# One chain of side stages through all scans, with spread loads and later transfers, in a four-layer scan and attention kernel

## The chip, the cores and the metric

The kernel runs on one core of a Trainium2 chip. A core has a matrix engine (TensorE, PE in the profile), three engines for elementwise work (VectorE or DVE, ScalarE or ACT, GpSimd or POOL), and SyncE (SP), which here issues nearly all transfers. Each engine takes its own instructions strictly in order and waits at an instruction until its semaphores allow it. The metric is the device time of one execution in microseconds (us); the median of several runs counts.

## The reference

The input `x` is 4 images of 96 channels and 64 by 64 pixels, in float32. Four layers follow each other for each image, each fed by a normalised copy of the running result and added to it:

- L0: attention of 3 heads from all 4096 pixels to 1024 pooled samples, a weighting of each pixel's 2 by 2 block by its 9 neighbouring samples, a 5 by 5 depthwise convolution and a projection.
- L1: a selective scan over the pixels in four orders, then a layer norm, a gate, 1x1, 3x3 depthwise and 1x1 convolutions, and a channel gate.
- L2: a 3 by 3 convolution with all 96 by 96 channels.
- L3: convolutions, again a selective scan in four orders, layer norms, a gate with a second branch, grouped convolutions and a softmax over channels.

The scans are the largest part. For each of 192 channels and 16 states, in each of four orders (rows, rows backwards, columns, columns backwards), both L1 and L3 compute, written as in L3,

```
step: h = h * exp(d[..., None] * A) + (d * uu)[..., None] * bb[:, :, None, :]
      y = einsum('bkdn,bkn->bkd', h, cc)
```

where `d`, `bb` and `cc` are themselves projections of the input at that pixel. The four orders' results are added. So there are 8 large scans: two layers by four images.

## The kernel before

The function `streams` does everything for these inputs (`general` is a second version that runs only where a range check fails). Its main loop runs through 8 scans in the order of `SCANS`: L1 of images 0 and 1, L3 of 0 and 1, L1 of 2 and 3, L3 of 2 and 3. A scan is cut into 32 groups (4 orders, or ways, x 4 chunks of 1024 pixels x 2 halves of 96 channels), and a group into `NG` = 12 units. A unit is a tile of 128 partitions (16 states x 8 channels) by 1024 pixels. There are 8 x 384 = 3072 units.

A unit `i` goes through the engines in steps, which the function `unit` emits for several units at once:

- `fetch` (L1964): SyncE loads the group's `dd` (the step sizes, stored to memory by `prepare`), repeated over the 16 states, into one of 12 `rep` buffers. It is emitted `AHEAD` = 4 units ahead.
- `decays` (L1971): ScalarE turns `rep` into exp(d*A), two units ahead.
- `drive` (L1978): TensorE spreads the group's `parts` into one of two `bx` tiles in PSUM (1024 columns), two units ahead; `times_b` (L1987): VectorE multiplies it by `bc`, one unit ahead.
- `scan` (L1991): VectorE runs the recurrence into `hs`; `carry_on`: ScalarE copies its last column to the next chunk's start.
- `times_c` (L2006): GpSimd multiplies `hs` by `bc` back into `rep`.
- `collect` (L2010): every fourth unit, TensorE sums the states of four units into `acc`, which takes one PSUM tile; after the last four of a group `output` (L2028) adds or copies `acc` into the tile `yo`, and its store to `y_row` or `y_col` is put into `store` and issued at the beginning of the next unit.

`prepare` (L1863) makes the inputs of a group two groups ahead, in steps that `unit` places one or two at a time: projections on TensorE, the softplus on ScalarE and GpSimd, and transfers through memory (`rows` to `bc`, `dd`, `du` to `parts`). Its transfers are emitted some units after the step that makes their data, through `later(n, f)`; it starts when `LEAD` = 6 units of a group are left.

Beside the scan, the same loop does the rest of the network. Each image has the stages `first` (L0 and the inputs of L1's scan), `second` (the rest of L1, L2 and the inputs of L3's scan), and `third` (the rest of L3); `last` is the `third` of the last image, which works while its own scan still runs. They are Python generators. A `Slots` object takes the next piece of a generator with `begin`, up to three times in a unit: before `decays`, between `times_b` and `collect`, and after `drive`. A piece is mostly some matmuls into a PSUM tile from `bank()`; where it yields `None`, `end` then emits what follows on the other engines, later in the same unit. TensorE's time of the pieces is estimated and subtracted from a budget: `PACE[s]` us per unit of scan `s`, less 0.43 for `drive` and 1.71 where `collect` is due. A piece that yields `WAIT` is not ready yet and takes the rest of that `begin`'s budget.

`BESIDE[s]` lists what runs beside scan `s`. A new `Slots` begins at each scan's first unit, and what is left of it 19 units before the scan's end is emitted at once. First(0) runs alone before the loop, and what is left of `last` after it: `solo` is true there, and the tiles of `bx` serve as banks.

PSUM has little room: `bx` 2 x 2 banks, `acc` 2 banks, and the tag `one` two banks, for `bank()` outside solo. `held()` takes one of these two for long: for the sums and weighted values in `attention`, the variance rows in `layer_norm`, the sums in `neighbours`. Meanwhile one bank is left for all pieces.

`directions` (L1440) begins `second` and `third`: for both halves it loads the column result `yc` and the row result `V` in 32 transfers of 96 KB, turns the columns with ScalarE (`turned`), and adds both on TensorE. `second` waits there (`stored[0] < full - 1 + h`) until its scan's stores are issued. `finish` (L1673) is the rest of `third` and `last`. In `group_norm_on_scalar` (L1095) ScalarE sums four pieces and VectorE reduces them; at L1619 and L1620 ScalarE's Tanh is followed by VectorE's product on the same bank; in `layer_norm` ScalarE's Sqrt is followed by VectorE's reciprocal.

## Time and profile before

| | before |
|---|---|
| median of 3 runs | 14276.35 us (14261.17 to 14285.1) |
| the profiled execution | 14250.58 us, its span 14248.7 us |
| PE, DVE, ACT, POOL busy | 81%, 82%, 61%, 72% |
| alone before the first unit, and after the last | 690.5 us, 127.4 us |
| scans 0 to 7 | 1660, 1646, 1630, 1604, 1590, 1624, 1633, 2044 us |
| transfers | 2694.85 MB, mean 189 GB/s |

Busy time is that of an engine's own instructions; issuing transfers and waiting for semaphores do not count. PEld is TensorE's weight load, which overlaps its matmuls. A row of the groups of instructions shows line, engine, operation, what is written and read, the count, then the busy time and the mean in ns, then the engine's idle time before them and what ended most of it. Windows give each engine's busy time in a stretch, with the granted TensorE clock (1.00 is full speed), the share of time in which the 16 DMA engines were busy, and GB/s. A row of waits names the waiting instruction, what ended its wait, the total in us, how often, and the longest. The helper `mm` issues every matmul, so all matmuls have its line, L964, and are told apart by their tiles.

### The profile page before, as it was taken

To read this page: it belongs to the slowest core of one execution; us is meant where nothing else is said; L and a number is where in the kernel's file an instruction comes from. 1 tells how busy PE (TensorE), PEld (TensorE's weight loads), DVE (VectorE), ACT (ScalarE), POOL (GpSimd) and SP (SyncE) were. 2 spreads that over 40 slices of the span, in tenths; PEclk is the share of its full clock that TensorE was granted. 3 is DMA by queue.
4 is the path that set the end of the run, shared out by engine and by line. 5 is a ranking of instruction groups with operands and counts; after the bars stand their busy time and mean duration, and the time that the engine had idled before them with its cause. 6 is when DMAs were issued, how large, how long until landed. Compare 5 with 4: busy or idle time off the path is not lost.

```text
span 14248.7 us, 127656 instructions
## 1 busy us (share of the span) xinstructions
PE 11588.7 (81%) x40137; PEld 3442.3 (24%) x40802; DVE 11635.9 (82%) x7509; ACT 8680.4 (61%) x12307; POOL 10197.3 (72%) x4637
## 2 busy tenths in 40 slices
PE   8878886988879796888868887988879797877767
PEld 2322321322213221222212221222213221211111
DVE  1478888987889888889988898897989888777786
ACT  3266566666756676665756566566756666655554
POOL 0167887877868777778877787787868777655573
PEclk9889887998879897999979997998879897777766
DMA  0267788787878888678977788787878878676684
GB/s 10 61 154 193 196 216 208 197 213 181 226 185 217 210 205 216 172 185 219 237 178 196 195 220 231 186 223 180 230 191 218 211 195 222 169 178 174 165 198 106
DMA packets 846672, 2694.85 MB, mean 189 GB/s; under 512 B 112480, under 2 KB 115008, under 8 KB 845984
## 3 DMA queue, kind: packets, MB, share of 16 engines
q1 hardware_dynamic: 845328, 2685.08, 74.9%
q8 instruction: 325, 5.32, 0.2%
q14 instruction: 363, 2.97, 0.1%
q10 hardware_dynamic: 656, 1.47, 0.0%
HBM read 2185.95 MB, written 500.17 MB: 189 GB/s over the span
## 4 chain that ended last, share of the span: by engine, by line
PE 36%; DVE 20%; ACT 15%; DMA 11%; issue 7%; POOL 7%; SPq 1%; DVEq 0%; POOLq 0%; ACTq 0%
PE one L964 24%; DVE hs L1996 12%; PE bx L964 6%; PE acc L964 6%; DVE bx L1989 6%; DMA rep<-dd 5%; ACT rep L1976 4%; POOL rep L2008 4%; ACT L1976 1%; DMA du<-cut 1%; PE held L964 1%; ACT ex L1309 1%; DMA parts<-du 1%; DMA yc<-ycol 1%; ACT L1918 1%
## 5 line engine op out<-in xcount | busy, mean ns | idle before, releaser
L2008 POOL TENSOR_TENSOR rep<-hs,bc 128x1024 f32<-128x1024 f32 x3072 | 7219.0, 2356 | 2792.8 <-DVE hs L1996 2410.8
L1996 DVE TENSOR_TENSOR_SCAN hs<-rep,carry,bx 128x1024 f32<-128x1024 f32 x2304 | 5401.2, 2344 | 301.6 <-ACT carry L2004 33.3
L1989 DVE TENSOR_TENSOR bx<-bx,bc 128x1024 f32<-128x1024 f32 x3072 | 3720.1, 1211 | 862.4 <-PE bx L964 616.7
L1976 ACT ACTIVATE rep<-rep,l_decay 128x1024 f32<-128x1024 f32 x3072 | 3497.0, 1143 | 879.3 <-DMA rep<-dd 851.6
L964 PE MATMUL bx<-parts,spread 128*128 128x512 bf16 x5479 | 1959.3, 434 | 1242.4 <-DVE hs L1996 1123.2
L1996 DVE TENSOR_TENSOR_SCAN hs<-rep,bx 128x1024 f32<-128x1024 f32 x768 | 1754.2, 2284 | 136.2 <-ACT carry L2004 56.1
L964 PE MATMUL acc<-rep,ct 128*32 128x512 f32 x12288 | 1833.1, 712 | 11.8 <-POOL rep L2008 8.7
L964 PEld LDWEIGHTS <-spread 128*128 128x128 bf16 x6144 | 458.6, 102 | 3655.5 <-DVE hs L1996 2239.6
L964 PE MATMUL one<-band,dg 96*96 96x512 f32 x2304 | 1067.0, 595 | 4.6 <-ACT band L1512 0.8
L964 PE MATMUL one<-upad,diag 96*96 96x512 f32 x2016 | 959.0, 607 | 6.9 <-ACT pr L1881 2.2
L964 PE MATMUL one<-qq,kk 96*128 96x512 f32 x1152 | 659.9, 656 | 201.4 <-ACT ex L1309 137.3
L964 PE MATMUL one<-pr,ct 6*96 6x512 f32 x1024 | 691.3, 761 | 69.9 <-ACT pr L1881 24.6
L964 PEld LDWEIGHTS acc<-rep,ct 128*32 128x32 f32 x12288 | 374.3, 123 | 1268.0 <-issue 1026.3
L1309 ACT ACTIVATE ex<-one 128x512 f32<-128x512 f32 x576 | 342.0, 594 | 548.5 <-PE one L964 547.0
L1976 ACT ACT_TABLE_LOAD x474 | 608.1, 1283 | 8.3
L964 PE MATMUL one<-hp,diag 96*96 96x512 f32 x1152 | 580.8, 641 | 35.6 <-POOL diag L1134 33.5
L964 PE MATMUL one<-vpad,diag 96*96 96x512 f32 x1200 | 579.2, 610 | 2.1
L2004 ACT COPY carry<-hs 128x1 f32<-128x1 f32 x2304 | 407.8, 177 | 225.5 <-DVE hs L1996 224.6
L964 PE MATMUL held<-ex,cols 128*32 128x256 f32 x3072 | 504.1, 404 | 18.1 <-ACT ex L1309 11.7
L964 PE MATMUL held<-ex,vT 128*32 128x256 f32 x3072 | 504.5, 405 | 0.0
L964 PEld LDWEIGHTS one<-band,dg 96*96 96x96 f32 x2304 | 368.8, 163 | 507.2 <-issue 426.1
L964 PEld LDWEIGHTS one<-upad,diag 96*96 96x96 f32 x2016 | 327.9, 165 | 456.3 <-issue 392.0
(3422 smaller groups left out, 14112.9 us busy)
## 6 DMA issues: line engine op xcount, KB each, us to landing
rep<-dd SPq DMA_DIRECT2D x3072, 512.0 KB
parts<-du SPq DMA_DIRECT2D x1024, 144.0 KB
bc<-rows SPq DMA_DIRECT2D x256, 512.0 KB
dd<-delta SPq DMA_DIRECT2D x256, 384.0 KB
du<-cut SPq DMA_DIRECT2D x256, 384.0 KB
yrow<-yo SPq DMA_DIRECT2D x128, 512.0 KB
ycol<-yo SPq DMA_DIRECT2D x128, 512.0 KB
us<-urow SPq DMA_DIRECT2D x128, 384.0 KB
```

The lines of the kernel that those rows point to most:

```text
L964: nc.tensor.matmul(o, lhsT=lhsT, rhs=rhs, start=first, stop=last)
L1309: nc.scalar.activation(last.rearrange("p a b -> p (a b)"), p, AF.Exp, scale=HD**-0.5)
L1918: nc.scalar.activation(w, w, AF.Ln)
L1976: nc.scalar.activation(a, a, AF.Exp, scale=decay[tag][:, k, NG * h + m : NG * h + m + 1])
L1989: nc.vector.tensor_mul(bx, bx, ready[i // NG][2][:, 0, :])
L1996: nc.vector.tensor_tensor_scan(out=hs, data0=a, data1=bx, initial=carry[:, h, m : m + 1] if c else 0.0, op0=ALU.mult, op1=ALU.add)
L2004: nc.scalar.copy(carry[:, h, m : m + 1], live[i][1][:, CH - 1 : CH])
L2008: nc.gpsimd.tensor_tensor(a, hs, ready[i // NG][2][:, 1, :], ALU.mult)
```

## The change

- `BESIDE`: third(0) and third(1) go beside scans 3 and 4, after first(2) and first(3). Beside scan 7 third(2) and `last` stay.
- The stages form one generator through all scans, in one `Slots`. A scan's end is no boundary: the next stage may begin in it. What is still open 19 units before a scan's end is emitted as before, but only up to the end of that scan's list (`done`).
- A clock counts units, and `stores` notes the unit in which each y store is issued. `landed(n)` is true two units after the n-th. `directions` first loads the image that is complete, in 8 transfers of 384 KB, one per unit, then the other one chunk by chunk as its stores land, 4 transfers of 96 KB per unit. `last` loads its columns in 8 transfers, one per unit.
- `WAIT` ends the stage's pieces for the rest of the unit but keeps the budget. It is new between ScalarE's sums and VectorE's reduction, after Sqrt in `layer_norm`, and after Tanh in `second`.
- `tight`: while a bank is held, no piece is placed between `times_b` and `collect`.
- `AHEAD` 4 to 6, `LEAD` 6 to 8; the transfers of `prepare` one unit later, the y store two units after its `output`.
- `PACE`: scans 3 and 4 from 2.95 to 3.5, the others by 0.03 up or down (scan 7 unchanged).

```diff
-          (("first", 3),), (("second", 2),), (("second", 3),), (("third", 0), ("third", 1), ("third", 2), ("last", 3)))
+BESIDE = ((("first", 1),), (("second", 0),), (("second", 1),), (("first", 2), ("third", 0)),
+          (("first", 3), ("third", 1)), (("second", 2),), (("second", 3),), (("third", 2), ("last", 3)))
-PACE = (2.95,3.45,3.45,2.95,2.95,3.45,3.45,3.2)
+PACE = (2.98, 3.42, 3.42, 3.5, 3.5, 3.42, 3.42, 3.2)
...
     def held():
+        tight[0] = True
...
+    clock, stores, tight, done = [0], [], [False], [0]
+    def landed(n):
+        return len(stores) >= n and clock[0] >= stores[n - 1] + 2
+    def scanned(tag, b, axis):
+        way = 2 * NCH
+        k = max(n for n, (_, a, _) in enumerate(KINDS[tag]) if a == axis)
+        return (4 * SCANS.index((tag, b)) + k) * way
...
             nc.scalar.activation(s, s, AF.Copy, accum_out=st[:, j : j + 1])
             yield 1
+        yield WAIT
...
         nc.scalar.activation(r[:m], acc[:m], AF.Sqrt, bias=eps[:m])
-        yield n
+        tight[0] = False
+        yield WAIT
...
-            full = len(groups) // len(SCANS) * (SCANS.index((tag, b)) + 1)
-            cols = []
+            cols = [T.tile([96, W, H], F32, name="yc", bufs=2) for h in range(2)]
+            flat = {"c": [t.rearrange("p a b -> p (a b)") for t in cols], "r": [V[:, h, :] for h in range(2)]}
+            image_of = {"c": y_col, "r": y_row}
+            soon, late = sorted("rc", key=lambda a: scanned(tag, b, a))
+            while not landed(scanned(tag, b, soon) + 2 * NCH):
+                yield WAIT
             for h in range(2):
-                while stored[0] < full - 1 + h:
+                for q in range(4):
+                    nc.sync.dma_start(out=flat[soon][h][24 * q : 24 * q + 24],
+                                      in_=image_of[soon][h][b][32 * q : 32 * q + 24, :])
                     yield WAIT
-                t = T.tile([96, W, H], F32, name="yc", bufs=2)
-                cols.append(t)
-                for j in range(4):
-                    ungapped(t.rearrange("p a b -> p (a b)")[:, bass.ts(j, CH)], y_col[h][b], bass.ts(j, CH))
-                    ungapped(V[:, h, bass.ts(j, CH)], y_row[h][b], bass.ts(j, CH))
-                yield 4
+            for c in range(NCH):
+                for h in range(2):
+                    while not landed(scanned(tag, b, late) + 2 * c + h + 1):
+                        yield WAIT
+                    js = bass.ts(NCH - 1 - c, CH)
+                    ungapped(flat[late][h][:, js], image_of[late][h][b], js)
+                    yield WAIT
+            yield WAIT
...
                     nc.scalar.activation(q[:96], q[:96], AF.Tanh, bias=half_ag2, scale=0.5)
+                    yield WAIT
                     nc.vector.scalar_tensor_tensor(out=x2, in0=q[:96], scalar=1.0, in1=x2, op0=ALU.add, op1=ALU.mult)
...
-            later(1, to_rows)
-            later(3, to_bc)
+            later(2, to_rows)
+            later(4, to_bc)
...
-        later(1, lambda: nc.sync.dma_start(out=dd, in_=delta))
+        later(2, lambda: nc.sync.dma_start(out=dd, in_=delta))
...
-        later(1, to_du)
-        later(3, to_parts)
+        later(2, to_du)
+        later(4, to_parts)
...
-    AHEAD, BEHIND, LEAD = 4, 2, 6
+    AHEAD, BEHIND, LEAD = 6, 2, 8
...
-        while store:
-            store.pop()()
-            stored[0] += 1
         catch_up(1)
...
-        left -= work.begin(left)
+        if not tight[0]:
+            left -= work.begin(left)
         if due:
             collect(j)
...
-            store.append(output(j))
+            later(2, stored(output(j)))
...
-            if left < 0.3:
+            if left < 0.3 or self.rest == clock[0]:
                 return 0.0
...
             if v == WAIT:
-                return left
+                self.rest = clock[0]
+                return 0.0
...
-    def beside(s):
+    def beside():
         stages = {"first": first, "second": second, "third": third, "last": last}
-        for n, b in BESIDE[s]:
-            yield from stages[n](b)
+        for s in range(len(SCANS)):
+            for n, b in BESIDE[s]:
+                yield from stages[n](b)
+            done[0] += 1
+    work = Slots(beside())
...
-            if at == 0:
-                work, owed = Slots(beside(s)), 0.0
+            clock[0] = i
...
             if at == per - NG - LEAD - 1 and s < len(SCANS) - 1:
-                work.run()
+                while done[0] <= s:
+                    work.begin(9.0)
+                    work.end()
```

`tight[0]` is set to false again where the held bank has been read: after Sqrt in `layer_norm`, after the last products in `attention`, after the reciprocal in `neighbours`.

## The prediction

> **What bounds the kernel now.** I read the page first, then busy time by scan, then inside scan 1 and scan 3, then the waits of VectorE and of SyncE's queue. The page:
>
> ```profile
> span 14248.7 us, 127656 instructions
> PE 11588.7 (81%) x40137; PEld 3442.3 (24%) x40802; DVE 11635.9 (82%) x7509; ACT 8680.4 (61%) x12307; POOL 10197.3 (72%) x4637
> L1996 DVE TENSOR_TENSOR_SCAN hs<-rep,carry,bx 128x1024 f32<-128x1024 f32 x2304 | 5401.2, 2344 | 301.6 <-ACT carry L2004 33.3
> L1989 DVE TENSOR_TENSOR bx<-bx,bc 128x1024 f32<-128x1024 f32 x3072 | 3720.1, 1211 | 862.4 <-PE bx L964 616.7
> ```
>
> Each of the 3072 units needs one scan and one product on VectorE: 2.34 + 1.21 = 3.55 us. The run of units lasts 13,431 us, 4.37 per unit. The windows by scan (solo start, scans 0, 1, 3, 4, 7, tail; columns: length, then busy us of PE, PEld, DVE, ACT, POOL, clock, DMA share, GB/s):
>
> ```profile
> 0.00:690.50 690.50, 603.53 (x2719) 217.91 (x2720) 180.77 (x285) 208.01 (x346) 38.16 (x46) 0.95 0.10 28
> 690.50:2350.90 1660.40, 1337.86 (x5460) 399.08 (x5556) 1399.95 (x852) 1030.10 (x1496) 1272.28 (x572) 0.86 0.78 195
> 2350.90:3996.90 1646.00, 1370.64 (x4254) 419.15 (x4332) 1400.97 (x868) 1053.67 (x1450) 1267.30 (x571) 0.87 0.81 203
> ...
> 5626.80:7231.10 1604.30, 1298.84 (x5472) 391.51 (x5568) 1409.78 (x861) 1012.84 (x1476) 1273.12 (x573) 0.89 0.81 203
> 7231.10:8821.40 1590.30, 1295.81 (x5472) 391.15 (x5568) 1403.84 (x854) 1023.67 (x1487) 1273.06 (x573) 0.89 0.80 203
> ...
> 12077.70:14121.30 2043.60, 1475.44 (x3861) 350.99 (x3932) 1596.75 (x1132) 1180.85 (x1680) 1266.53 (x593) 0.74 0.69 173
> 14121.30:14248.70 127.40, 86.06 (x130) 21.15 (x130) 29.04 (x41) 23.34 (x40) 4.86 (x3) 0.62 0.12 36
> ```
>
> VectorE works 11,636 - 181 - 29 = 11,426 us inside the scans; the remaining 2,005 us are its idle time. No VectorE instruction disappears, so only these 2,005 us can be won. Scan 7 holds 447 of them, scan 0 260, the others 186 to 245. Where they lie, in scan 1 (directions; c2 convolutions; gate and group norm; the stretch with Tanh; bare units at the end) and in scan 3 (attention):
>
> ```profile
> 2350.90:2447.40 96.50, 63.57 (x177) 18.27 (x181) 58.86 (x38) 56.08 (x81) 56.30 (x25) 0.80 0.79 197
> 2587.30:3062.40 475.10, 463.66 (x1541) 156.97 (x1568) 449.51 (x261) 306.15 (x450) 417.30 (x183) 1.00 0.89 220
> 3062.40:3152.20 89.80, 43.10 (x143) 11.67 (x145) 64.59 (x50) 60.16 (x83) 55.27 (x33) 0.67 0.83 217
> 3279.10:3484.00 204.90, 161.89 (x465) 46.37 (x472) 144.77 (x89) 135.13 (x185) 133.31 (x59) 0.87 0.61 154
> 3812.50:3996.90 184.40, 102.09 (x317) 18.29 (x321) 168.09 (x98) 100.08 (x126) 153.81 (x68) 0.61 0.88 224
> ```
> ```profile
> 5672.10:6311.10 639.00, 543.78 (x2921) 160.29 (x2969) 531.83 (x323) 412.64 (x645) 474.62 (x206) 0.92 0.75 184
> ```
>
> By their scans these are 16, 128, 16, 40, 47 and 145 units: 6.03, 3.71, 5.6, 5.1, 3.92 and 4.41 us each. TensorE at full clock beside VectorE (the second) is near the floor; units without side work are no faster. So compressing stages costs little, and the bad stretches are waits (waits of the engines, then of SyncE's queue; us in total, times, longest):
>
> ```profile
> DVE bx L1989 <- PE bx L964: 616.7, 313, 17.4
> DVE x L1620 <- ACT one L1619: 92.0, 28, 7.7
> DVE gs_mv L1103 <- ACT X L1100: 50.3, 5, 12.8
> ACT rep L1976 <- DMA rep<-dd: 851.6, 439, 14.2
> ```
> ```profile
> SPq L2044 <- DVE yo L2035: 1300.5, 114, 26.0
> SPq L2044 <- ACT yo L2037: 775.4, 61, 26.2
> ```
>
> SyncE stands 2,850 us before y stores (four rows of L2044, two shown), with fetches queued behind; ScalarE then waits for `rep`, TensorE for ScalarE, VectorE for `bx`.
>
> **What the Trainium skill says.** "DMA: Bandwidth & Descriptors", Rules for kernel authors: issue a DMA early and wait late, so its fixed cost overlaps. The trace agrees: `rep` pieces of about 10 us lie on the chain that ended last (4.8% of the span), against a lead of two units, 7 to 8 us. "TensorE: Matmul & The Clock Gate", What's actually happening: the clock follows recent activity. Here it is 1.00 in the convolutions, 0.61 in bare units. "Perfetto Trace Analysis", Optimization Strategy: interleave regimes with different limits. Scan 7 at clock 0.74 beside scans 3 and 4 at 0.89 fits.
>
> **The change, part by part.** Units are counted in the changed program's order.
>
> *Loads spread.* `directions` issued 64 DMAs in a burst, about 0.42 us each on SyncE: 27 us. The seven stretches took about 679 us for 110 units, 6.2 each. Now 40 DMAs go out over 16 units, in the bare end of the previous scan for the second stages; `directions` spans 317 units. I take 4.05 each. Bounds: 3.85 (bare), and 4.4, since 384 KB per unit on top of about 870 KB (2,685 MB / 3072) may fill DMA engines already at 0.88.
>
> *Fetch six ahead, y store and transfers later.* Lead of `rep` goes from two units to four, about 15 us, above the 10 us pieces. The y store comes two units after its sum, so SyncE no longer stands there. Twelve `rep` buffers remain: a fetch now reuses one released in the unit before (three units before, formerly). Behind it SyncE queues `dd`, `du`, `parts` and side loads. `parts` still leaves at most two units before its first product, so faster units make this hand-over tighter. Net 0 to 200 us; I count it inside the stage rates.
>
> *Middle slot closed while a bank is held.* `held` takes one of two `one` banks; a middle piece then puts TensorE behind ScalarE's Exp, just ahead of `drive`. VectorE needs 531.83/145 = 3.67; I take 4.0 against 4.41, because two steps per unit (about 1.3 us each by the solo start's pace, plus 0.86 for `drive` and `collect`) give TensorE 3.5 us, under 3.55. Bounds 3.75 and 4.4.
>
> *WAIT after Tanh, sums, Sqrt.* They move VectorE's next step one unit on: up to 92 (`x`) + 50 and 18 (`gs_mv` after `X` and `xn`) + 26 (`ln_r`) us in the waits of VectorE. I count 23 + 12 per second stage. Nothing urgent stands behind the postponed step; a stage only gets longer by a few units.
>
> *Third stages moved, PACE.* Thirds 0 and 1 leave scan 7 and take units 256 to 351 of scans 3 and 4, since `first` at 3.5 finishes by 256. A third's `finish` took about 1,114 us for 206 units, 5.4; denser pacing cannot repair its gate (Silu then product). I keep 5.3. In scan 7 `last` has its columns turned by unit 117 and then waits for the last way's stores, so about 200 units become bare, 3.75 each (178.0 us for 48 units between 13,565 and 13,743).
>
> Sums (units x us):
> Scan 0: group norm 10x4.9, attention 145x4.0, neighbours 17x5.2, convolutions 96x3.9, norm and in_conv 80x4.0, directions 36x4.05 = 1557 (1660 before).
> Scans 1, 2, 5, 6: directions 19x4.05, layer norm 21x5.6, middle 252x3.92, in_conv 59x3.88, end 33x4.0 = 1544 (1633 on average).
> Scans 3, 4: attention 100x4.0, neighbours 16x5.2, convolutions 75x3.8, norm 10x4.3, in_conv 55x3.8, directions 28x4.05, finish 67x5.3, end 33x4.05 = 1622 each (1604, 1590).
> Scan 7: directions 20x4.05, finish 73x5.35, turn 24x4, bare 200x3.75, last 67x5.2 = 1666 (2044).
> With the start 690 and a tail of 132 (stores seen later leave slightly more for it): 690 + 1557 + 4x1544 + 2x1622 + 1666 + 132 = 13,465 us of span. The profiled execution took 14,250.6, its span plus 2; the runs' median is 26 above, so I forecast 13,490.
>
> **Rivals.**
> *Stalls re-form.* Waits leave ScalarE and SyncE but come back at `drive` and `parts`: attention stays at 4.3, directions 4.3, middle 4.05, finish 5.6: 393x0.3 + 317x0.25 + 1008x0.13 + 207x0.3 = 390 us more, about 13,880. For it: followed back over the 8 us before each, 695 of some 1,046 us of VectorE's idle time before `bx`, `hs` and `yo` show no longer DMA piece. Against: the convolutions run at 3.71 with the same `drive`.
> *Everything to the floor.* Attention 3.75, directions 3.9, middle 3.8, finish 5.0: 98 + 48 + 121 + 62 = 330 less, about 13,160. Against: DMA share 0.88 to 0.92 at 3.7 us per unit leaves little room.
> *Slower.* The `rep` ring: in one unit of four SyncE stands before the fetch until `collect` of the unit before has been read by TensorE; all its transfers wait there. There are 768 such groups; if each costs VectorE more than 1.0 us, the 785 us forecast are eaten, and at 1.5 us the time is about 14,640. Against: four units of lead lie between fetch and use.
> *Only moved.* Scans 3 and 4 grow by what scan 7 loses and bursts merely spread: about 14,270.
>
> **How the numbers follow.** Chances: forecast 0.6, stalls re-form 0.2, floor 0.13, slower 0.05, only moved 0.02. Ends of the bounds: attention (3.75 to 4.4) -98 to +157, directions -63 to +111, middle -121 to +131. The range reaches from the floor case to the re-formed stalls: 13,130 to 13,880. Within 0.2% of the median (29 us) lies about what a measurement of this kernel can tell from no change: faster 0.94, same 0.01, slower 0.05.
>
> **What would show it.** Right: scans 3 and 4 near 1,600 us, scan 7 near 1,670, scan 0 down by 100; `x` L1620's wait (a new line) gone; attention at about 4 us per unit; ScalarE's wait for `rep` far under 850 us; no y-store rows of 1,300 us on SyncE. Wrong: SyncE waiting for `acc` at the fetches with VectorE waiting for `bx`; `directions` above 4.4; third stages above 6 us per unit beside `first`.

## The result, and the profile after

The change makes the kernel slower: 14,630.86 us (median; 14,613.01 to 14,651.25) against 14,268.76 us for the kernel before on the same chip, a ratio of 1.0258, 95% interval 1.0233 to 1.0284. The forecast was 13,490 us, with a range of 13,130 to 13,880: the time moved the other way. The profiled execution took 14,636.66 us.

From the page of the kernel after: its span, the busy time of the engines, and VectorE's two steps of every unit (busy us, mean ns, then idle time just before and its largest releaser):

```profile
span 14634.8 us, 127626 instructions
PE 11741.7 (80%) x40154; PEld 3477.8 (24%) x40802; DVE 11633.1 (79%) x7509; ACT 8689.6 (59%) x12307; POOL 10206.2 (70%) x4637
L2022 DVE TENSOR_TENSOR_SCAN hs<-rep,carry,bx 128x1024 f32<-128x1024 f32 x2304 | 5401.9, 2345 | 306.6 <-ACT carry L2030 32.8
L2015 DVE TENSOR_TENSOR bx<-bx,bc 128x1024 f32<-128x1024 f32 x3072 | 3718.7, 1211 | 1066.5 <-PE bx L964 617.9
```

VectorE's work is the same (11,633 us, before 11,636), and so are its durations. All of the 386 us of span are new idle time of VectorE: inside the scans it is idle for 2,399 us, before 2,005. The idle time ahead of the product with `bc` went from 862 to 1,067.

The same kernel by scan (scans 0, 3, 4 and 7; length, then busy us of PE, PEld, DVE, ACT, POOL, clock, DMA share, GB/s):

```profile
689.40:2399.70 1710.30, 1360.92 (x5462) 407.77 (x5556) 1397.17 (x851) 1039.50 (x1501) 1273.90 (x573) 0.84 0.76 193
...
5716.20:7624.50 1908.30, 1560.83 (x5863) 460.21 (x5961) 1473.25 (x951) 1132.50 (x1649) 1277.68 (x583) 0.84 0.69 178
7624.50:9518.50 1894.00, 1515.23 (x5567) 435.58 (x5660) 1455.20 (x923) 1103.45 (x1579) 1273.80 (x574) 0.82 0.71 180
...
12809.90:14511.40 1701.50, 1088.26 (x3092) 229.27 (x3148) 1471.58 (x950) 948.24 (x1335) 1259.50 (x572) 0.69 0.74 189
```

| us | before | forecast | after |
|---|---|---|---|
| scan 0 | 1660 | 1557 | 1710 |
| scans 1, 2, 5, 6 | 1646, 1630, 1624, 1633 | 1544 each | 1642, 1675, 1642, 1649 |
| scans 3, 4 | 1604, 1590 | 1622 each | 1908, 1894 |
| scan 7 | 2044 | 1666 | 1701 |
| attention: scan 0, units 24 to 155; scans 3 and 4, units 0 to 95; per unit | 4.42; 4.61 | 4.0 | 4.69; 5.03 |
| units 352 to 383 and the next 32, together (mean over the starts of scans 1, 2, 5, 6) | 313 | 278 | 307 |

The forecast of 278 is 32 x 4.0 + 19 x 4.05 + 13 x 5.6. The two attention figures of scans 3 and 4 are not for the same work: paced at 3.5, their first 96 units hold 162 attention steps (one Exp each), before 108. Scan 7 gave what was expected of it, within 35 us. Scans 3 and 4 took 608 us more than before, scan 7 342 less. The other scans kept their old length or grew.

The waits of the kernel after (us in total, times, longest), first of the engines, then of SyncE's queue:

```profile
DVE bx L2015 <- PE bx L964: 617.9, 270, 24.8
ACT rep L2002 <- DMA rep<-dd: 278.8, 86, 11.8
PE bx L964 <- DMA parts<-du: 158.1, 11, 29.2
DVE x L1646 <- ACT one L1644: 104.7, 24, 7.3
PE one L964 <- DMA us<-ucol: 82.1, 4, 23.5
```
```profile
SPq L1994 <- PE acc L964: 5007.6, 598, 28.2
SPq L2070 <- DVE yo L2061: 41.2, 6, 36.8
```

Two waits went as planned: the y stores no longer hold SyncE (41 us for VectorE, 1,300 before), and ScalarE waits 279 us for `rep` (852). But SyncE now stands 5,008 us before its fetches (L1994) until TensorE has summed the four units (one `collect`) that hold the buffer they reuse; it was 611. All of SyncE's waits beside the scans together have hardly changed, about 10,200 us against 9,900: they stand at other instructions. And TensorE has few but long waits for `parts` and `us`.

### The profile page after: what moved, and what is told of

It reads as the page before. It is cut to its first block, busy times and chain, and to the rows that moved or that the text cites. A ratio compares the mean times of both kernels' runs of the same rounds, so it can differ in the third digit from the quotient of the medians.

```text
span 14634.8 us, 127626 instructions
## 1 busy us (share of the span) xinstructions
PE 11741.7 (80%) x40154; PEld 3477.8 (24%) x40802; DVE 11633.1 (79%) x7509; ACT 8689.6 (59%) x12307; POOL 10206.2 (70%) x4637
## 4 chain that ended last, share of the span: by engine, by line
PE 39%; DVE 23%; ACT 14%; DMA 8%; POOL 7%; issue 6%; SPq 1%; DVEq 0%; POOLq 0%; another core or an unknown queue 0%; ACTq 0%
PE one L964 26%; DVE hs L2022 15%; PE bx L964 6%; DVE bx L2015 6%; PE acc L964 6%; POOL rep L2034 3%; ACT rep L2002 3%; DMA rep<-dd 2%; PE held L964 2%; ACT L2002 1%; ACT ex L1324 1%; ACT L1944 1%; DMA V<-yrow 1%; DMA yc<-ycol 1%; DMA xz<-gate 0%
## 5 line engine op out<-in xcount | busy, mean ns | idle before, releaser
L964 PE MATMUL one<-qq,kk 96*128 96x512 f32 x1152 | 732.2, 721 | 166.0 <-ACT ex L1324 123.2
L964 PE MATMUL one<-pr,ct 6*96 6x512 f32 x1024 | 598.6, 667 | 50.6 <-ACT pr L1907 15.4
L2002 ACT ACT_TABLE_LOAD x474 | 608.1, 1283 | 8.3
L964 PE MATMUL one<-us,wt 96*38 96x512 f32 x1024 | 314.1, 742 | 168.8 <-DMA us<-ucol 82.1
```

The costliest lines, as they stand in the source:

```text
L964: nc.tensor.matmul(o, lhsT=lhsT, rhs=rhs, start=first, stop=last)
L2002: nc.scalar.activation(a, a, AF.Exp, scale=decay[tag][:, k, NG * h + m : NG * h + m + 1])
```

## The experiments

All ratios are times over the time of the kernel before, run on the same chip; the changed kernel is at 1.0258. A unit's place in its group is counted from 0 to 11; `collect` falls in units 1, 5 and 9.

**The rep ring in the changed kernel.** The trace pointed first to SyncE's 5,008 us. Two runs loosened the ring.

```diff
-    AHEAD, BEHIND, LEAD = 6, 2, 8
+    AHEAD, BEHIND, LEAD = 4, 2, 8        # e1_lead4
```


> The changed kernel with fetches four units ahead again; everything else of the change stays. Theory (rep ring: SyncE stands 5,008 us before fetches until TensorE has read the group whose buffers they reuse, and transfers, loads and stores queue behind): that wait falls below 1,000 us (611 before the change), and the time falls by 250 to 400 us, to 14,230 to 14,380. Rival (side work crowds scans 3 and 4 and the beginnings of the directions stages, whatever SyncE does): the wait falls, the time stays within 60 us of 14,631.


```diff
-        rep = sp.tile([128, CH], F32, name="rep", bufs=12)
+        rep = sp.tile([128, CH], F32, name="rep", bufs=13)   # e2_rep13
```


> The changed kernel with thirteen rep buffers in place of twelve, still six units ahead: a fetch reuses a buffer read two units before, no longer one unit before. Theory (rep ring): a third to two thirds of the 5,008 us of SyncE's wait go, and the time falls by 100 to 300 us, to 14,330 to 14,530. Rival (crowded side work): within 60 us of 14,631. If the lead of six itself is worth something once SyncE isn't held, this run is no slower than the one with a lead of four.

Measured: 1.0211 (1.0188 to 1.0233) with four ahead, 1.0194 (1.0177 to 1.0211) with thirteen buffers. SyncE's wait at the fetches fell to 1,249 and 2,617 us. Three quarters of that wait bring 0.5%, half of it 0.6%: the ring costs something, but most of the loss is elsewhere, and the size of SyncE's wait doesn't measure it. The wait didn't vanish either. SyncE now stood 1,622 and 1,504 us before the store to `dd` (19 in the changed kernel), and 1,156 and 202 us before the y stores; its waits still add up to about 10,200 us in both runs.

**Third stages and middle slot.**

```diff
-PACE = (2.98, 3.42, 3.42, 3.5, 3.5, 3.42, 3.42, 3.2)
+PACE = (2.95, 3.45, 3.45, 2.95, 2.95, 3.45, 3.45, 3.2)      # e3_thirds7, with BESIDE as before
```


> The changed kernel with the third stages back in scan 7 and the old pacing (2.95, 3.45, 3.2); leads, stores, loads and the closed middle slot stay as changed. Theory (crowded side work): scans 3 and 4 fall from 1,908 and 1,894 us to about 1,610 each, scan 7 rises from 1,701 to about 2,045: 14,390. Rival (rep ring alone): the neighbouring scans cost the same wherever the third stages are, so scans 3 and 4 lose about what scan 7 gains, the total within 60 us of 14,631.


```diff
-        if not tight[0]:
-            left -= work.begin(left)
+        left -= work.begin(left)                             # e4_middle
```


> The changed kernel with the middle slot of a unit open for side work always, as before the change; all else stays. My forecast had the closed slot save 0.4 us per attention unit (393 units, 157 us), so 14,790 without it. Rival (closing it pushes the next piece beside the following one, and TensorE comes late to drive: attention in scan 0 went from 4.57 to 4.85 us per unit): 0.3 us per unit less, about 120 us, so 14,510. If neither, within 60 us of 14,631.

Measured: 1.0176 (1.0159 to 1.0194) with the third stages back, 1.0218 (1.0199 to 1.0236) with the slot open. In the first, scans 3 and 4 took 1,682 and 1,577 us and scan 7 2,037. In the second, attention in scan 0 stayed at 4.68 us per unit. Scans 3 and 4 together took 3,795 us with the slot open, 3,802 with it closed. Neither theory on the slot holds: closing it didn't win the 157 us of the forecast, and it isn't what slowed this attention. The intervals allow that it costs nothing.

**Early loads.**

```diff
-                for q in range(4):
-                    nc.sync.dma_start(out=flat[soon][h][24 * q : 24 * q + 24],
-                                      in_=image_of[soon][h][b][32 * q : 32 * q + 24, :])
-                    yield WAIT
+                for c in range(NCH):                         # e5_small_loads
+                    js = bass.ts(c, CH)
+                    ungapped(flat[soon][h][:, js], image_of[soon][h][b], js)
+                    yield WAIT
```


> The changed kernel with the first half of the directions loads in pieces of 96 KB (24 partitions x 4 KB, four per unit) in place of one piece of 384 KB (24 partitions x 16 KB) per unit: the same bytes per unit, smaller pieces. Theory (large pieces fill the queue: units 352 to 367 take 5.9 us in the changed kernel, bare ones 3.65, and single units there 12 to 27 us, waiting for parts and us): those units fall to about 4.4 us, so 7 stretches x 16 units x 1.5 us = 170 us less, ratio 1.014. Rival (the bytes per unit decide): units 352 to 367 stay at 5.5 to 6.2 us and the ratio within 0.4% of 1.0258.


```diff
+                while not landed(scanned(tag, b, late) + 2 * NCH - 1 + h):
+                    yield WAIT
+                for c in range(NCH):                         # e7_burst, in place of all spread loads
+                    js = bass.ts(c, CH)
+                    ungapped(flat["c"][h][:, js], y_col[h][b], js)
+                    ungapped(flat["r"][h][:, js], y_row[h][b], js)
+                yield 4
```


> The changed kernel with the directions loads in one burst, as before the change: after the last y store of the scan, all 64 pieces of 96 KB at once, so in the first units of the next scan; all else stays. By my forecast the burst costs 2.1 us more on 317 units: ratio 1.05 or more. Rival (the loads cost the same wherever they lie: the 32 units after the boundary and the 32 before it together are 70 us over the bare rate in both kernels): ratio within 0.4% of 1.0258. Theory (the early loads are the cause of the loss): ratio below 1.015.

Measured: 1.0222 (1.0194 to 1.0249) with small pieces, not told apart from the changed kernel by the intervals, and 1.0177 (1.0148 to 1.0205) with the burst. The size of the pieces is not the point; their place is. The last and first 32 units around a scan's end (the row in the table) took 313 us in the kernel before, 307 in the changed kernel, and 292 with the burst put back. What spread loads do there is seen in TensorE's timeline of the kernel after, at the end of scan 1 (start, duration, operation, idle time before it):

```profile
3926.76 0.59 PE L964 MATMUL bx<-parts,spread 128*128 128x512 bf16 x1 [17.73 <-DMA parts<-du]
...
3971.32 3.64 PE L964 MATMUL one<-us,wt 96*38 96x512 f32 x8 [23.42 <-DMA us<-ucol]
```

The `parts` of that group were issued from 3,910.7 to 3,914.3 us, among the `V` loads, and the product that needs them started 12.5 us later. VectorE stood still for most of that time: two units of this stretch took 16 and 27 us. The next group's `us`, the first of a new scan, is needed one unit after it is emitted, and SyncE was behind by then: it issued the `us` from 3,962.4 us on, behind 16 of the 96 KB loads since 3,940.9. The two places recur. Of the five scan ends before scans 1, 2, 5, 6 and 7, four have a unit of 15 to 17 us, 25 units before the end, and all five one of 21 to 29 us, 18 before it. With small pieces the same two places take 14 to 16 and 18 to 28 us. With the burst neither stands out, and single units take up to 14 us there instead: TensorE's waits for `us`, 137 us in the whole changed kernel, are nearly gone, while those for `parts` add up to 160 us, as in the changed kernel (158).

**The issue times, and what they hide.** In both runs `dd`, `du` and `parts` move like `rows` and `bc`; `put` counts the store when it is issued.

```diff
-            later(2, to_rows)
-            later(4, to_bc)
+            later(1, to_rows)
+            later(3, to_bc)
...
-    AHEAD, BEHIND, LEAD = 6, 2, 8
+    AHEAD, BEHIND, LEAD = 4, 2, 6        # e6_times_undone
...
-            later(2, stored(output(j)))
+            later(1, stored(output(j)))
```


> The changed kernel with all issue times as before the change: fetches four ahead, preparing six units ahead, transfers one and three units later, the y store in the next unit. Loads, third stages, pacing, closed slot and waits stay as changed. Theory (later issue costs by itself, through parts and us that land late): ratio about 1.010, 200 us below the changed kernel. Rival (issue times matter only through the rep ring, which the run with a lead of four opened for 0.5%): ratio 1.019 to 1.023.


```diff
-            later(1, to_rows)
-            later(3, to_bc)
+            later(2, to_rows)
+            later(4, to_bc)
...
-    AHEAD, BEHIND, LEAD = 4, 2, 6
+    AHEAD, BEHIND, LEAD = 6, 2, 8        # e8_times_alone, on the kernel before
...
-            store.append(output(j))
+            later(2, put(output(j)))
```


> The kernel before with the issue times of the change alone: fetches six ahead, preparing eight units ahead, transfers two and four units later, the y store two units after its sum. My forecast counted 0 to 200 us of gain for this: ratio 0.986 to 1.000. Theory (rep ring): SyncE's wait for TensorE before fetches rises from 611 us to about 5,000 and the ratio is 1.005 to 1.015. Rival (the ring is harmless by itself): the wait rises, the ratio stays within 0.3% of 1.

Measured: 1.0122 (1.0094 to 1.0149) undone, 1.0041 (1.0029 to 1.0054) alone. Taken alone, the times made scans 1, 2, 5 and 6 shorter by 44 us together, and the scans with attention longer: its units rose from 4.42 to 4.72 in scan 0. One unit of a group, number 0, took 8.2 us there on average. SyncE's wait at fetches grew in the shorter scans too (438 us in scan 1, 676 in scan 0), so the ring alone can't be the cause. Of the times, one moves work of TensorE and ScalarE: `LEAD`, the unit in which `prepare` begins (with eight, it also moves the point at which a scan's leftovers are emitted from 19 to 21 units before its end). ScalarE in the changed kernel, at such a place (units 60 to 62), then TensorE and VectorE there:

```profile
1011.78 1.28 ACT L1944 ACT_TABLE_LOAD   x1
1013.07 1.06 ACT L1944 ACTIVATE w__4252<-w__4252 96x1024 f32<-96x1024 f32 x1
1014.14 1.28 ACT L2002 ACT_TABLE_LOAD   x1
...
1016.58 0.59 ACT L1324 ACTIVATE ex<-one 128x512 f32<-128x512 f32 x1
```
```profile
1013.11 0.38 PE L964 MATMUL held<-ex,cols 128*32 128x256 f32 x1
...
1017.22 2.07 PE L964 MATMUL one<-qq,kk 96*128 96x512 f32 x2 [3.17 <-ACT ex L1324]
1019.22 0.64 PE L964 MATMUL held<-ex,cols 128*32 128x256 f32 x1
```
```profile
1024.32 1.23 DVE L2015 TENSOR_TENSOR bx<-bx,bc 128x1024 f32<-128x1024 f32 x1 [5.07 <-PE bx L964]
```

`prepare`'s Ln (L1944) stands between two loads of ScalarE's function table, one for it and one for the Exp that follows: together they take ScalarE for 3.6 us. "ScalarE: Activation LUTs" of the Trainium skill, What ACT_TABLE_LOAD costs, gives 1283 ns for a load, as here, but some 2.66 us in all, with a drain; in this trace the next instruction starts 0.01 us after the load, so 1.28 is the whole price. Attention's Exp (`ex`) stands behind that, TensorE waits 3.17 us for it with the next step's matmuls, and two steps stand ahead of the next `drive`. After the wait the same matmul takes 0.64 us, before it 0.38. In the attention of scan 0 (units 24 to 155, 11 groups) TensorE waits over 2 us for `ex` 11 times in the changed kernel, once per group and each time within 7 us after an Ln has begun; in the kernel before it does so 4 times, again after an Ln. Started eight units ahead, Ln lies in unit 10, and units 10, 11 and 0 have about two attention steps each. Started six ahead it lay in unit 0, ahead of unit 1 with its `collect` and one step at most. Three runs tried this.

```diff
-    AHEAD, BEHIND, LEAD = 4, 2, 6
+    AHEAD, BEHIND, LEAD = 4, 2, 8        # e9_prepare8, on the kernel before
```


> The kernel before with one number changed: a group is prepared eight units ahead, no longer six (fetches four ahead, transfers and y store as before). Theory (phase of the preparation: its Ln with two table loads, 3.6 us of ScalarE, then falls in unit 10 of 12, with two attention steps in each of units 10, 11 and 0, instead of just ahead of unit 1, which has one): the attention of scan 0 rises from 4.42 to about 4.7 us per unit, units 0 of a group to about 8 us, and the ratio is 1.004 to 1.008. Rival (the six fetches and the late transfers cost it): attention stays at 4.4, ratio within 0.2% of 1.


```diff
-    AHEAD, BEHIND, LEAD = 6, 2, 8
+    AHEAD, BEHIND, LEAD = 6, 2, 9        # e10_prepare9, on the kernel of e8_times_alone
```


> The kernel before with the issue times of the change (fetches six ahead, transfers two and four units later, y store two units after its sum), but prepared nine units ahead instead of eight, which puts Ln into unit 9 of a group, the one with collect and so at most one attention step. Theory (phase): attention of scan 0 back to 4.4 to 4.5 us per unit from 4.72, and with the 10 to 20 us that scans 1, 2, 5 and 6 gained from the times the ratio is 0.993 to 0.999. Rival (rep ring): SyncE still waits about 4,700 us before fetches, attention stays at 4.7, ratio 1.003 to 1.006.


```diff
-    AHEAD, BEHIND, LEAD = 6, 2, 8
+    AHEAD, BEHIND, LEAD = 6, 2, 10       # e11_after_prepare10, on the changed kernel
```


> The changed kernel with one number changed: prepared ten units ahead, no longer eight, which puts Ln into unit 8 of a group, ahead of unit 9 with collect. Theory (phase): attention of scans 0, 3 and 4 falls by 0.25 us per unit or more, 345 units, so 90 to 150 us less, ratio 1.015 to 1.020. Rival: ratio within 0.3% of 1.0258.

Measured: 1.0140 (1.0114 to 1.0167) for preparing eight ahead alone, 0.9977 (0.9968 to 0.9985) for all the times with nine, 1.0117 (1.0091 to 1.0142) for the changed kernel with ten. The first is well above the 1.004 to 1.008 that the phase was expected to cost. Setting this one number to ten in the changed kernel brings as much as undoing all its issue times (1.0122): of the 228 us between the two profiles 172 lie in scans 0, 3 and 4, the ones with attention. The attention of scan 0, units 24 to 155, in the kernel before with eight ahead, then with the times and nine ahead:

```profile
838.20:1465.20 627.00, 532.13 (x2792) 146.65 (x2790) 484.44 (x287) 376.42 (x574) 435.48 (x189) 0.87 0.69 172
```
```profile
847.30:1439.00 591.70, 505.01 (x2790) 142.64 (x2783) 484.81 (x286) 370.92 (x569) 436.29 (x189) 0.91 0.73 182
```

132 units at 4.75 and 4.48 us, with the same work. The slowest unit of a group moves with Ln: unit 3 (6.1 us) in the kernel before with Ln in unit 0, unit 0 (8.3) with Ln in unit 10, unit 11 (7.1) with Ln in unit 9. In the changed kernel with ten no unit stands out like this (at most 6.0). Of the 35 us between the two lines only 8 are idle time of TensorE. The other 27 are busy time: the same matmuls take longer, at a clock of 0.87 against 0.91. With nine ahead TensorE still waits for `ex` after every Ln, but for 2.3 to 3.3 us, with eight ahead for 3.0 to 3.7. So a wait seems to cost TensorE more than its own length here. Two things stay open: all steps of `prepare` move with `LEAD`, and no run moves Ln alone; and no run changes the clock without the waits.

**Is it the phase, and what is left of the ring?**

```diff
-    AHEAD, BEHIND, LEAD = 4, 2, 6
+    AHEAD, BEHIND, LEAD = 4, 2, 9        # e13_prepare9_alone, on the kernel before
```


> The kernel before, prepared nine units ahead instead of six, nothing else (fetches four ahead, transfers one and three units later, y store in the next unit). Theory (phase): Ln lies in unit 9 of a group, so the 1.4% that eight units ahead cost alone are gone: ratio 0.997 to 1.003. Rival (earlier preparation costs by itself, and the six fetches made up for it): ratio 1.010 or more.


```diff
-        rep = sp.tile([128, CH], F32, name="rep", bufs=12)
+        rep = sp.tile([128, CH], F32, name="rep", bufs=13)   # e14_prepare9_rep13, on e10_prepare9
```


> The kernel before with the issue times of the change, prepared nine ahead (ratio 0.9977 with twelve rep buffers), and thirteen rep buffers. If the rep ring still costs (SyncE waits 3,915 us for TensorE before fetches in that kernel): SyncE's wait falls to about 2,000 us and the ratio is 0.990 to 0.995. If it is harmless: the wait falls and the ratio stays at 0.996 to 0.9995.


```diff
-    AHEAD, BEHIND, LEAD = 6, 2, 9
+    AHEAD, BEHIND, LEAD = 5, 2, 9        # e18_prepare9_rep13_lead5, on e14_prepare9_rep13
```


> The kernel before with the issue times of the change, prepared nine units ahead, thirteen rep buffers and fetches five ahead, no longer six: a fetch reuses a buffer released two to three units before. If what is left of SyncE's wait (3,157 us) still costs: 0.981 to 0.985. If the ring is now loose enough: within 0.2% of 0.9872. If the sixth unit of lead carried the gain: 0.990 or more.

Measured: 1.0098 (1.0080 to 1.0115) for nine ahead alone, close to the rival's 1.010: of the 1.4% that eight units ahead cost alone, the phase is 0.4, and 1.0 comes with preparing earlier in either phase. Attention came back in scan 0 (4.49) and half way in scans 3 and 4, but the total didn't. Its waits of SyncE, and ScalarE's wait for `rep` there:

```profile
SPq L1968 <- PE acc L964: 1963.0, 285, 23.2
SPq L1924 <- POOL delta L1921: 1345.4, 197, 21.2
```
```profile
ACT rep L1976 <- DMA rep<-dd: 977.1, 459, 19.1
```

Against the kernel before, SyncE stands 1,345 us before `dd` until GpSimd has made `delta` (288 before), and ScalarE waits 977 us for `rep` (852). With the issue times of the change this wait of ScalarE is 122 us and the ratio 1.2% lower. Late fetches are thus what an earlier preparation meets when `dd` is issued one unit after its step; that they cost the whole 1.0% is argued from these waits, not shown.

Thirteen buffers give 0.9872 (0.9856 to 0.9889), 14,115 us, 1.05% below the same kernel with twelve: here the ring is worth more than in the changed kernel. SyncE's wait at the fetches fell only from 3,915 to 3,157 us. Of the 134 us between the two profiles, 51 lie in the first 32 units of scans 1, 2, 5 and 6, where the `directions` loads go out in a burst (5.84 us per unit in scan 1 with twelve buffers, 5.44 with thirteen), and 49 in their units 160 to 223, where SyncE also issues loads and stores of the second stage; the attention of scan 0 didn't change (4.48). One unit less of lead at thirteen buffers gave 14,132.5 us against 14,115 (0.9915, 0.9898 to 0.9931, by a kernel before that ran 0.25% faster on that chip): SyncE's wait fell to 2,004 us, and there is no further gain. In time the two runs differ by 0.1%, in ratio by 0.4%; as they ran on two chips, what the sixth unit of lead is worth stays open.

**The other parts at the better phase.** Three runs on the changed kernel with ten units of preparation and the slot open.

```diff
-PACE = (2.98, 3.42, 3.42, 3.5, 3.5, 3.42, 3.42, 3.2)
+PACE = (2.95, 3.45, 3.45, 2.95, 2.95, 3.45, 3.45, 3.2)      # e12_waits; BESIDE as before, loads as in e7_burst
...
-    AHEAD, BEHIND, LEAD = 6, 2, 8
+    AHEAD, BEHIND, LEAD = 6, 2, 10
...
-        if not tight[0]:
-            left -= work.begin(left)
+        left -= work.begin(left)
```


> The changed kernel without four of its parts: third stages back in scan 7 with the old pacing, directions loads in a burst, middle slot open always, and preparation ten units ahead. What is left is the later fetches, transfers and stores, the chain of stages through all scans and the waits after Tanh, the sums and Sqrt. If the parts add up (third stages 0.8%, burst 0.8%, slot 0.4%, phase 0.7%, of 2.6%) the ratio is 0.996 to 1.003. If they don't, because a stall that one part takes away comes back at the next, 1.008 or more.


```diff
-PACE = (2.95, 3.45, 3.45, 2.95, 2.95, 3.45, 3.45, 3.2)
+PACE = (2.98, 3.42, 3.42, 3.5, 3.5, 3.42, 3.42, 3.2)        # e15_thirds_moved, on e12_waits; BESIDE as changed
```


> The changed kernel prepared ten units ahead, with directions loads in a burst and the middle slot always open; the third stages lie beside scans 3 and 4 with the pacing of the change. Against the run with the third stages back in scan 7 (ratio 1.0025, all else equal) this gives their cost at the better phase. Theory (scans 3 and 4, paced at 3.5, lose more than scan 7 gains): 1.008 to 1.013. Rival (the move only looked dear beside the bad phase): within 0.2% of 1.0025 or below. By my forecast: 1.5% below it.


```diff
-                    ungapped(flat["c"][h][:, js], y_col[h][b], js)
-                    ungapped(flat["r"][h][:, js], y_row[h][b], js)
+                for q in range(4):
+                    nc.sync.dma_start(out=flat[soon][h][24 * q : 24 * q + 24],
+                                      in_=image_of[soon][h][b][32 * q : 32 * q + 24, :])
+                    yield WAIT                               # e16_early_loads, on e12_waits, and so on as changed
```


> The changed kernel prepared ten units ahead, with the third stages in scan 7 and the middle slot always open; the directions loads are spread over the end of the scan before, as the change has them. Against the run with the burst (ratio 1.0025, all else equal) this gives the cost of the early loads at the better phase. Theory (they delay parts and us at the end of each scan: single units of 12 to 27 us): 1.006 to 1.012. Rival (a burst costs as much where it was): within 0.2% of 1.0025. By my forecast: 1.5% below it.

Measured: 1.0025 (1.0014 to 1.0035), 1.0034 (1.0025 to 1.0044) and 1.0053 (1.0030 to 1.0075). Scans 3, 4 and 7 with the third stages in scan 7, then moved:

```profile
5654.90:7296.90 1642.00, 1371.42 (x5996) 414.26 (x5994) 1414.53 (x863) 1038.21 (x1520) 1273.85 (x572) 0.90 0.79 198
7296.90:8832.70 1535.80, 1223.77 (x4714) 346.77 (x4710) 1382.82 (x827) 951.11 (x1347) 1265.54 (x563) 0.84 0.83 209
12175.40:14161.70 1986.30, 1430.70 (x3748) 322.81 (x3746) 1556.15 (x1082) 1095.97 (x1583) 1256.36 (x580) 0.72 0.69 173
```
```profile
5629.30:7517.10 1887.80, 1602.47 (x6480) 479.76 (x6480) 1477.60 (x957) 1161.20 (x1703) 1277.85 (x583) 0.88 0.71 180
7517.10:9269.20 1752.10, 1416.67 (x5076) 399.49 (x5072) 1448.84 (x917) 1062.79 (x1513) 1272.80 (x574) 0.83 0.76 191
12478.40:14179.90 1701.50, 1140.14 (x3148) 234.29 (x3148) 1473.75 (x950) 950.05 (x1335) 1256.87 (x571) 0.68 0.77 192
```

Scans 3 and 4 lose 462 us by the move, scan 7 wins 285, and the other scans win 160, of which 116 in scan 6, where the chain of the first run already begins a third stage. Here side work costs about the same wherever it lies. The 0.8% seen before came with the bad phase, the closed slot and the spread loads together; which of these makes the move dear was not tried. The early loads cost 0.28%, between the two branches of what was expected. The parts don't add up: undone one by one, preparation, third stages, loads and slot bring 1.4, 0.8, 0.8 and 0.4%, in sum 3.4; undone together (1.0025) 2.3. The difference is barely clear of the intervals, and the run met its expected range only because that reckoned with 0.7 for the preparation. The kernel before with the later times and nine ahead had 0.9977, so what else is left in the first run, the chain of stages, the waits and ten units instead of nine, brings no gain; how the 0.5% between the two is shared was not tried.

**Both corrections in the changed kernel.**

```diff
-    AHEAD, BEHIND, LEAD = 6, 2, 8
+    AHEAD, BEHIND, LEAD = 6, 2, 10       # e17_after_both
...
-        rep = sp.tile([128, CH], F32, name="rep", bufs=12)
+        rep = sp.tile([128, CH], F32, name="rep", bufs=13)
```


> The changed kernel with two numbers changed: prepared ten units ahead (alone: 1.0117) and thirteen rep buffers (alone: 1.0194). Theory (phase and ring are the loss, and add up): 1.0117 - 0.0064 to 1.0117 - 0.0105, so 1.001 to 1.006. Rival (the early loads, the third stages beside the attention and the closed slot keep a loss of their own, and the ring costs nothing beside them): 1.009 to 1.013.

Measured: 1.0058 (1.0036 to 1.0079). Two numbers account for 2.0 of the 2.6%, and thirteen buffers bring 0.6% at this phase as at the other (1.0258 to 1.0194). The last 0.6% is shared by the parts that stay: the spread loads cost 0.28% by the runs above, with an interval that reaches down to nothing; the slot and the waits were not separated.

## Why the prediction was wrong

The forecast named the floor correctly: VectorE's durations and its work didn't move, and only its idle time could change. It then let 785 us of that idle time go, and 394 came instead. By scan the span of 14,635 misses the sum of 13,465 by 153 us in scan 0, 432 in scans 1, 2, 5 and 6, 558 in scans 3 and 4, 35 in scan 7 and -9 in the tail.

Two things have to be kept apart. That the kernel became slower is explained for the most part by two numbers, the lead of the preparation and the size of the ring: with both put right it is at 1.0058. That the forecast gain didn't come is not: this kernel still spans 14,314 us, 143 us too much in scan 0, 318 in scans 1, 2, 5 and 6, 379 in scans 3 and 4 and 16 in scan 7. There the stage rates failed. The attention of scan 0 in the kernel after (units 24 to 155):

```profile
851.70:1471.20 619.50, 532.41 (x2759) 148.54 (x2804) 482.07 (x286) 375.78 (x576) 431.95 (x188) 0.87 0.69 174
```

- **"Fetch six ahead, y store and transfers later": net 0 to 200 us.** This is the step that failed first. It priced the moved transfers and put at nothing that `prepare` itself begins two units earlier. Its instructions on ScalarE, Ln with two table loads among them, were never placed in their unit. Alone the earlier begin costs 1.4%, and setting it to ten in the changed kernel brings 1.4%. What the step did price was of the right sign: with preparation at eight or nine units, the later times are worth 1.0 to 1.2% (1.0140 to 1.0041, 1.0098 to 0.9977).
- **"Against: four units of lead lie between fetch and use."** The argument against the rival of the rep ring looked at the fetched unit alone. A fetch that waits also holds what stands behind it on SyncE: `parts`, `us` and the loads, which have no four units. The gains of a thirteenth buffer agree with this; that it works by these transfers is argued. The rival's time, 14,640, was nearly met, but its mechanism made a part: 0.5 to 0.6% in the changed kernel, 1.05% in the kernel with nine ahead.
- **"Loads spread": 6.2 to 4.05, bounded at 4.4.** The bound counted bytes against bandwidth. The 64 units around a scan's end went from 313 to 307 us, where 278 were forecast. At each of these ends TensorE waits once for a late `parts` (8 to 22 us) and once for a late `us` (17 to 25 us). A mean rate doesn't have such waits, and together they are more than the 29 us of the miss.
- **"Middle slot closed": attention at 4.0.** Measured 4.69 and 5.03. The term that was too small is TensorE's own time: two steps per unit were to "give TensorE 3.5 us, under 3.55". The forecast's own line for the attention of scan 3 has 543.78 us of TensorE in 145 units, 3.75 each, which is already above the 3.67 of VectorE. The 3.5 were reckoned at the pace of the solo start, whose clock is 0.95. In the changed kernel the line above gives 532.41 us in 132 units, 4.03 each at a clock of 0.87; in scans 3 and 4, with half as many steps again in a unit, it is 4.43 in the first 96 units, at 0.88. With TensorE's time at these clocks, 4.0 was out of reach even without a wait; whether the clock would be higher without the waits is not shown. At the better phases scan 0 is at 4.4 to 4.5, with the slot closed (ten ahead) as with the slot open. On top of TensorE's work comes the way through ScalarE's Exp back to TensorE, in which `prepare`'s turns on ScalarE lie. (The bounds of this term were also counted over 393 units, where the sums have 345; this moves each end by under 20 us.)
- **"WAIT after Tanh, sums, Sqrt": 23 + 12 us per second stage.** The wait at the sums went as planned, from 68 us (`gs_mv` after `X` and `xn`) to 26. The other two stayed: 104.7 us at Tanh (L1646), before 92.0, and 24 us after Sqrt, before 26. The step is one unit later, yet it comes at that unit's start; that this is the reason is argued. The middle of scans 1, 2, 5 and 6 (units 32 to 351) stayed at 4.18 us per unit, before 4.13; the forecast had (1544 - 278) / 320 = 3.96. Why these stretches stayed, with SyncE's waits for the y stores gone, is not shown.
- **"Third stages moved".** Right in scan 7 and in the place of the third stages. In scans 3 and 4 the units 256 to 350 took 5.82 us each, where directions at 4.05 and `finish` at 5.3 make 4.93. Of the scans' excess of 558 us this is 169, and the first 96 units, at 5.03 instead of 4.0, are 198: the attention that was packed more densely to make room was not counted as dearer. The rates of the third stages were taken from scan 7; with the burst, the open slot and ten units ahead the same units took 5.03 us, near the forecast, so it is not their place alone that makes them dear. The other 191 us lie in the rest of these scans. The rival "Only moved" describes this part.

Of the signs that the forecast named for being wrong, two stand in the trace of the kernel after: SyncE waiting for `acc` at the fetches, and directions above 4.4 (5.5 to 5.9 in the sixteen units of the loads, 4.7 in the first twenty of the next scan). The third stages, at 5.82, stay just under the 6 us that were named.

The best kernel of this study is the one before with later transfers, preparation nine units ahead and thirteen `rep` buffers: 0.9872 of the time before.

## What to carry to other kernels

When a schedule constant is changed, list every instruction it moves on every engine and the unit it lands in: here one unit's difference in the place of the preparation, with a ScalarE step of 3.6 us in it, was worth 0.4 and 0.6% in two kernels, and two units' difference 1.4% in the third. Count TensorE's own time from the trace of the stage that it is forecast for, at that stage's clock. A longer lead over the same number of buffers takes its slack from the ring, and the issuing engine's wait only moves: what counts is which transfers stand behind it. A bound on spread loads needs the latest transfer that a product waits for, not the mean rate.

## What the runs showed of the hardware

A switch of ScalarE's table took 1.28 us and nothing more (474 loads at one line, of 1,283 ns each; the next instruction followed after 0.01 us). After a wait of 3.17 us TensorE's matmuls of one form took 0.64 us, before it 0.38; over an attention stage with such a wait in every group the clock was 0.87, and 0.91 where the waits were shorter. Transfers of 144 KB issued among 384 KB loads, with the DMA engines 0.92 busy (3,910 to 3,927 us of the kernel after), took 12.5 us until their product could start, and splitting the loads into 96 KB pieces left units of 14 to 28 us at the same places. And a smaller wait of the issuing engine at one instruction is no measure of a gain: SyncE's wait at the fetches fell by 758 us for 1.05% in one kernel, and by 3,759 us for 0.5% in another, where its waits in all stayed at about 10,200 us.
